# The rows of B and C of a selective scan: one tile and one load, or two

## The chip, the cores and the metric

The kernel runs on one core of a Trainium2 chip. The metric is the device time in microseconds (us). The engines are named as the profile names them: PE (matrix multiply), DVE (vector), ACT (scalar functions), POOL (GpSimd) and SP, whose queue issues most of the DMAs. Each engine works through its own queue in order, and waits on semaphores for what the other engines or DMAs have to deliver.

## The reference

Four layers run on 4 images of 64 x 64 tokens with 128 channels, all in 32-bit floats: a Mamba-like block with a selective scan in four directions (layer 0), self-attention over all tokens (layer 1), a convolution block (layer 2) and neighborhood attention with an MLP (layer 3). The change lies in the scan of layer 0:

```python
B, H, W, C = (4, 64, 64, 128)
DI, N, R, K = (256, 16, 8, 4)
xs = jnp.stack([x0, x1, x0[..., ::-1], x1[..., ::-1]], axis=1)      # four directions
x_dbl = jnp.einsum('bkdl,kcd->bkcl', xs, x_proj_w)
dts, Bs, Cs = jnp.split(x_dbl, [R, R + N], axis=2)
delta = jax.nn.softplus(jnp.einsum('bkrl,kdr->bkdl', dts, dt_w) + dt_b[None, :, :, None])
A = -jnp.exp(A_log).reshape(K, DI, N)
def step(h, t):
    x_t, d_t, B_t, C_t = t
    h = jnp.exp(d_t[..., None] * A) * h + (d_t * x_t)[..., None] * B_t[:, :, None, :]
    return (h, jnp.einsum('bkdn,bkn->bkd', h, C_t))
```

For each image and direction there are 256 channels x 16 states, each a linear recurrence over 4096 tokens. B scales what goes into the state, and C weighs the 16 states into the output.

## The kernel before, in words

The program is written for a framework that schedules it: it orders the instructions of every engine by priority and by a model of time, inserts the semaphores, and hands out tiles from pools. A tile name with bufs=4 has four buffers in turn; the instruction that writes the fifth tile waits for the last reader of the first.

**Inputs of the scan.** `scan_inputs` computes delta, du (delta times x, on POOL, L328) and the rows of B and C, and writes them to DRAM scratch: delta (L326), du (L332), and `D.bc` (L325), which holds for each of the 16 states n one row of B and one row of C of 512 tokens side by side (shape [16, 2, 512]).

**The scan.** `selective_scan` runs over an image. Its loops are, from outside in: the direction k (4, in the order 0, 1, 3, 2), the chunk of 512 tokens i (8), the half of the channels hf (2), the group of four states j (4), and pp (2). A tile has 128 partitions, 32 channels times 4 states. One pass of the innermost loop is a unit: 512 units in an image, 2048 in all. For each half, two dt tiles (delta) and two du tiles are loaded (L468, bufs=4), each copied to the four states. For each j, one bc tile is loaded (L476, bufs=4): B in its first 512 columns and C in its second, copied to the 32 channels. A unit is then:

- dB = du x B on POOL (L485), for two groups g of channels at once, into one of four buffers;
- for each g: dA = exp(delta A) on ACT into PSUM (L491, three buffers), and the recurrence on DVE (L493, tensor_tensor_scan), into dA or hc;
- the product with C: on DVE for each g (L498), or, in 5 of 16 units of the first image and in 7 of 16 of the others (`ON_POOL`), on POOL for both g at once (L506), put behind by two units (`BEHIND`, a list called `waiting`) so that POOL doesn't wait for the scan;
- the last column copied as the state for the next chunk, on ACT (L500, L502).

When both units of a j are made, PE sums over the states with a 128 x 32 matrix of ones (`pick`, L539) into py. At the first j of a half, py is begun with the skip term (L524, for which y_before is loaded from xc in two halves at L520) or with what earlier directions gave (L527 and L534, loads L526 and L530). At the last j ACT copies py to y_sum and stores it (L549 to L558).

**What runs beside it.** The scan of image b+1 has the highest priority. Beside it run the other layers of image b (`rest`: scan_output, layers 1 and 2, layer 3), and beside the first image's scan the inputs of the images to come. What is left of the last image runs when its scan is over. On each engine the instructions of both are in one queue.

Loads, of the scan and of the other layers, are issued by SP in one order. The load of a bc tile waits until its buffer's last reader, a product on DVE or POOL, is done; what stands behind it on SP waits too.

Of the kernel before, what the change touches and what calls it, by code (L numbers as in the profile page):

```python
# [28 lines left out]
F32 = mybir.dt.float32  # L29
# [13 lines left out]
LC = 512  # L43
# [20 lines left out]
def bc(ap, shape):  # L64
    return ap.to_broadcast(list(shape))


def mid(ap, n):

    return bc(ap.unsqueeze(1), [ap.shape[0], n, ap.shape[1]])  # L70


def span(c, n=LC):
    return slice(c * n, (c + 1) * n)
# [12 lines left out]
def after(tc, later, earlier, kind=mybir.DependencyClass.Sync):  # L87
    tc.add_manual_dep(
        later.ins, earlier.ins.name, mybir.DependencyInfo(kind, mybir.DependencyReason.DATA), reason="group"
    )  # L90
# [347 lines left out]
def selective_scan(tc, K, S, D, img):  # L438

    nc = tc.nc
    pool, psum = S.pool, S.psum
    waiting = []

    def settle(unit):
        while waiting and waiting[0][0] <= unit:
            waiting.pop(0)[1]()

    for k in ORDER:
        back = k >= 2
        order = slice(None, None, -1) if back else slice(None)
        last = 0 if back else LC - 1
        state = pool.tile([128, NJS, NPR, 2], F32, name="state")
        for i in range(NCH):  # L460
            c = NCH - 1 - i if back else i
            for hf in range(2):
                dts, dus = [], []
                for pp in range(2):
                    rows = span(2 * hf + pp, 32)
                    for name, src, out in (("dt", D.delta, dts), ("du", D.du, dus)):
                        t = pool.tile([128, 2, LC], F32, name=name, bufs=4)
                        nc.sync.dma_start(  # L468
                            t.rearrange("p g t -> p (g t)"),
                            src[img][k][c][rows].rearrange("d g t -> d (g t)").unsqueeze(1).to_broadcast([32, 4, 2 * LC]),  # L470
                        )
                        out.append(t)
                py = []
                for j in range(NJS):
                    bct = pool.tile([128, 2, LC], F32, name="bc", bufs=4)
                    nc.sync.dma_start(  # L476
                        bct.rearrange("p g t -> p (g t)"),
                        D.bc[img][k][c][4 * j : 4 * j + 4].rearrange("n w t -> n (w t)").unsqueeze(0)
                        .to_broadcast([32, 4, 2 * LC]),
                    )  # L480
                    hcs, made = [], []
                    for pp in range(2):
                        pr = 2 * hf + pp
                        dB = pool.tile([128, 2, LC], F32, name="dB", bufs=4)
                        nc.gpsimd.tensor_mul(dB, dus[pp], mid(bct[:, 0, :], 2))  # L485
                        on_pool = S.unit % 16 in ON_POOL[img > 0]
                        S.unit += 1
                        hc = pool.tile([128, 2, LC], F32, name="hc", bufs=6)
                        for g in range(2):
                            dA = psum.tile([128, LC], F32, name="dA", bufs=3)  # L490
                            nc.scalar.activation(dA, dts[pp][:, g, :], AF.Exp, scale=S.A[:, k, j, pr, g : g + 1])  # L491
                            hg = hc[:, g, :] if on_pool else dA
                            nc.vector.tensor_tensor_scan(  # L493
                                hg[:, order], dA[:, order], dB[:, g, order],
                                0.0 if i == 0 else state[:, j, pr, g : g + 1], ALU.mult, ALU.add,
                            )
                            if not on_pool:
                                mm = nc.vector.tensor_mul(hc[:, g, :], dA, bct[:, 1, :])  # L498
                                if i < NCH - 1:
                                    nc.scalar.copy(state[:, j, pr, g : g + 1], dA[:, last : last + 1])  # L500
                        if on_pool and i < NCH - 1:
                            nc.scalar.copy(state[:, j, pr, :], hc[:, :, last])  # L502
                        if on_pool:

                            def product(hc=hc, bct=bct, made=made):
                                made.append(nc.gpsimd.tensor_mul(hc, hc, mid(bct[:, 1, :], 2)))  # L506

                            waiting.append((S.unit + BEHIND, product))
                        else:
                            made.append(mm)  # L510
                        hcs.append(hc)
                        settle(S.unit)

                    def total(k=k, c=c, hf=hf, j=j, hcs=hcs, made=made, py=py):
                        if j == 0:
                            py.append(psum.tile([128, LC], F32, name="py"))
                            before = pool.tile([128, LC], F32, name="y_before", bufs=3)
                            if k == 0:
                                for pp in range(2):
                                    nc.sync.dma_start(  # L520
                                        before[span(pp, 64), :],
                                        D.xc[img][c][span(2 * hf + pp, 32)].rearrange("d g t -> g d t"),
                                    )
                                nc.tensor.matmul(py[0], S.skip[:, hf, :], before, start=True, stop=False)  # L524
                            elif k >= 2:
                                nc.sync.dma_start(before, D.y_first[img][k % 2][c][:, hf, :])  # L526
                                nc.tensor.matmul(py[0], K.ident, before, start=True, stop=False)  # L527
                            if k == 2:
                                cols = pool.tile([128, NCH, RC, RC], F32, name="y_before", bufs=3)
                                nc.sync.dma_start(  # L530
                                    cols.rearrange("p c a b -> p c (a b)"),
                                    D.y_cols[img][:, :, c, hf].rearrange("c p x -> p c x"),
                                )
                                nc.tensor.matmul(  # L534
                                    py[0].rearrange("p (a c b) -> p a c b", a=RC, b=RC), K.ident,
                                    cols.rearrange("p c a b -> p a c b"), start=False, stop=False,
                                )
                        for q in range(4):
                            mm = nc.tensor.matmul(  # L539
                                py[0][32 * q : 32 * q + 32, :], S.pick, hcs[q // 2][:, q % 2, :],  # L540
                                start=(k == 1 and j == 0), stop=(j == NJS - 1),
                            )
                            if q == 0:
                                for m in made:
                                    after(tc, mm, m)
                        if j == NJS - 1:
                            y = pool.tile([128, LC], F32, name="y_sum")
                            if k == 3:
                                nc.scalar.copy(  # L549
                                    y.rearrange("p (b a) -> p b a", b=H), py[0].rearrange("p (a b) -> p b a", b=H)  # L550
                                )
                                nc.scalar.dma_start(
                                    D.y_cols[img][c][:, :, hf, :], y.rearrange("p (r x) -> p r x", r=NCH)
                                )
                            else:
                                nc.scalar.copy(y, py[0])
                                to = D.y[img][c] if k == 2 else D.y_first[img][k % 2][c]
                                nc.scalar.dma_start(to[:, hf, :], y)  # L558

                    waiting.append((max([S.unit] + [w[0] for w in waiting]), total))  # L560
                    settle(S.unit)
    settle(S.unit + BEHIND)
# [1194 lines left out]
```

## Time and profile before

| | |
|---|---|
| device time, median of 3 runs | 8969.41 us (8967.38 to 8976.73) |
| the profiled execution | 8980.37 us |
| its span | 8978.6 us |
| busy PE / DVE / ACT / POOL | 7201.0 / 7114.0 / 5647.9 / 7046.0 us |
| mean rate of the DMAs | 176 GB/s |
| loads of bc (L476) | 1024 of 512 KB |
| loads of dt and of du (L468) | 512 of each, 512 KB |
| mean of a dB multiply (L485) and of a POOL product (L506) | 2363 ns each |
| mean of a DVE product (L498) | 677 ns |

The profile is of one execution. A row of a group has the line, the engine, the operation with its output and inputs, the count, the busy time in us with the mean in ns, and the idle time of the engine just before these instructions with what ended most of it. A row of waits has the waiting engine and line, what it waited for, the total in us, how often, and the longest. "SPq" is the issue of a DMA by SP's queue. A row of windows has the stretch in us, its length, the busy time of each engine with the instructions begun, the clock granted to PE, the share of time that the DMA engines were busy, and GB/s. A row of the timeline has the start and the duration in us, and in brackets the idle time of the engine before it and what ended it.

### The profile page before, as it was taken

The page shows a single profiled execution, that of the slowest core. Times are in us where ns is not written, and L with a number is a line of the kernel's source. Part 1 is how long each engine was busy: PE and PEld are TensorE (multiplying, and loading weights), DVE is VectorE, ACT ScalarE, POOL GpSimd, SP SyncE. Part 2 cuts the span into 40 slices and gives each one's busy share as a digit, 9 for nine tenths or more (in the row PEclk, how much of TensorE's full clock was granted, in tenths as well). Part 3 has the DMA queues.
Part 4 walks back from the last instruction along what each step waited for, and adds up shares of the span by engine and source line. Part 5 has one row for each costly group of instructions (what it writes and reads, how often), then busy time and mean ns, then how long its engine had stood idle before and what let it go on. Part 6 is the DMA issues. An engine that isn't in the chain of part 4 may idle for free. (4 is left out here: it accounts for less than half of the span.)

```text
span 8978.6 us, 99358 instructions
## 1 busy us (share of the span) xinstructions
PE 7201.0 (80%) x30116; PEld 2731.9 (30%) x30116; DVE 7114.0 (79%) x8483; ACT 5647.9 (63%) x11581; POOL 7046.0 (78%) x3064
## 2 busy tenths in 40 slices
PE   5835868686788997888788888777888988888987
PEld 2211213132422232334322233333222333343333
DVE  3888878787899989988899989888899889833433
ACT  5746767676666666657766666667666666564355
POOL 5988898999899979998799979988899889910000
PEclk8756878696889998888899988888899988899988
DMA  5777666777544446565444555565444455520020
GB/s 169 250 239 235 240 244 233 253 251 265 184 166 161 167 151 211 194 212 186 152 166 172 179 180 183 193 205 176 166 161 168 160 200 190 192 74 4 7 79 29
DMA packets 716655, 1581.74 MB, mean 176 GB/s; under 512 B 203317, under 2 KB 328396, under 8 KB 711757
## 3 DMA queue, kind: packets, MB, share of 16 engines
q1 hardware_dynamic: 585805, 1399.10, 45.7%
q10 hardware_dynamic: 130304, 176.19, 5.6%
q8 instruction: 241, 3.95, 0.2%
q14 instruction: 305, 2.50, 0.1%
HBM read 1280.47 MB, written 283.59 MB: 174 GB/s over the span
## 5 line engine op out<-in xcount | busy, mean ns | idle before, releaser
L485 POOL TENSOR_TENSOR dB<-du,bc 128x1024 f32<-128x1024 f32 x2048 | 4790.4, 2363 | 687.8 <-DMA bc<-bc_dram 238.9
L491 ACT ACTIVATE dA<-dt,w_A_log 128x512 f32<-128x512 f32 x4096 | 2783.0, 691 | 607.6 <-DVE hc L493 298.0
L493 DVE TENSOR_TENSOR_SCAN dA<-dA,state,dB 128x512 f32<-128x512 f32 x2128 | 2631.7, 1273 | 291.0 <-POOL dB L485 158.2
L493 DVE TENSOR_TENSOR_SCAN hc<-dA,state,dB 128x512 f32<-128x512 f32 x1456 | 1805.5, 1269 | 299.3 <-ACT dA L491 116.6
L506 POOL TENSOR_TENSOR hc<-hc,bc 128x1024 f32<-128x1024 f32 x832 | 1963.0, 2363 | 83.5 <-ACT state L502 59.2
L498 DVE TENSOR_TENSOR hc<-dA,bc 128x512 f32<-128x512 f32 x2432 | 1568.7, 677 | 127.5 <-PE py L539 111.8
L539 PE MATMUL py<-hc,pick 128*32 128x512 f32 x8192 | 1252.5, 690 | 385.6 <-POOL hc L506 279.7
L829 PE MATMUL pa<-e,l_v 128*128 128x512 f32 x2048 | 1080.8, 660 | 28.8 <-ACT e L785 28.6
L500 ACT COPY state<-dA 128x1 f32<-128x1 f32 x2128 | 329.0, 158 | 1219.0 <-DVE hc L498 1207.7
L781 PE MATMUL pair<-l_g,l_f 32*128 32x512 f32 x2048 | 540.5, 679 | 185.9 <-ACT e L785 133.0
L785 ACT ACTIVATE e<-pair 128x1024 f32<-128x1024 f32 (+1 forms) x448 | 508.3, 1135 | 228.6 <-PE pair L781 222.3
L829 PEld LDWEIGHTS pa<-e,l_v 128*128 128x128 f32 x2048 | 379.8, 202 | 694.7 <-issue 635.1
L539 PEld LDWEIGHTS py<-hc,pick 128*32 128x32 f32 x8192 | 212.6, 116 | 1146.2 <-issue 448.0
L1287 PE MATMUL pair<-table,ident 128*128 128x512 f32 x768 | 424.4, 680 | 114.3 <-ACT e L1297 93.9
L247 PE MATMUL ps<-band,w_conv_diag 128*128 128x504 f32 (+3 forms) x1152 | 500.0, 593 | 3.5 <-ACT delta L397 3.5
L493 DVE TENSOR_TENSOR_SCAN dA<-dA,dB 128x512 f32<-128x512 f32 x304 | 357.7, 1213 | 71.2 <-POOL dB L485 52.2
L328 POOL TENSOR_TENSOR du<-delta,xc 128x1024 f32<-128x1024 f32 x128 | 333.1, 2610 | 48.4 <-ACT delta L397 46.9
L201 PE MATMUL ps<-ident,ln_xn 128*128 128x128 f32 x512 | 135.5, 360 | 289.4 <-ACT ln_xn L198 213.3
L1297 ACT ACTIVATE e<-pair 128x1024 f32<-128x1024 f32 (+1 forms) x224 | 254.4, 1136 | 154.9 <-PE pair L1291 154.5
L219 PE MATMUL ps<-xnT,w_fc_w 128*128 128x512 f32 x512 | 276.2, 674 | 69.3 <-ACT mlp_h L226 24.4
L781 PEld LDWEIGHTS pair<-l_g,l_f 32*128 32x128 f32 x2048 | 141.7, 191 | 548.9 <-ACT e L785 272.3
L247 PEld LDWEIGHTS ps<-band,w_conv_diag 128*128 128x128 f32 x1152 | 221.5, 193 | 282.0 <-issue 262.6
(274 smaller groups left out, 8562.9 us busy)
## 6 DMA issues: line engine op xcount, KB each, us to landing
bc<-bc_dram SPq DMA_DIRECT2D x1024, 512.0 KB
dt<-delta_dram SPq DMA_DIRECT2D x512, 512.0 KB
du<-du_dram SPq DMA_DIRECT2D x512, 512.0 KB
delta_dram<-delta ACTq DMA_DIRECT2D x128, 512.0 KB
du_dram<-du SPq DMA_DIRECT2D x128, 512.0 KB
table<-biasT_dram SPq DMA_DIRECT2D x72, 512.0 KB
y_first_dram<-y_sum ACTq DMA_DIRECT2D x128, 256.0 KB
y_before<-y_first_dram SPq DMA_DIRECT2D x128, 256.0 KB
```

What stands on the lines that cost most here:

```text
L247: mm = nc.tensor.matmul(out[:, r0 - row0 : r1 - row0, c0:c1], lhsT((dy + 1) * 3 + dx + 1), src[:, r0 + dy : r1 + dy, c0 + dx : c1 + dx], s ...
L328: nc.gpsimd.tensor_mul(du.rearrange("p d (a b) -> p d a b", b=H), deltas[b].rearrange("p d (a b) -> p d a b", b=H), tk,)
L485: nc.gpsimd.tensor_mul(dB, dus[pp], mid(bct[:, 0, :], 2))
L491: nc.scalar.activation(dA, dts[pp][:, g, :], AF.Exp, scale=S.A[:, k, j, pr, g : g + 1])
L493: nc.vector.tensor_tensor_scan(hg[:, order], dA[:, order], dB[:, g, order], 0.0 if i == 0 else state[:, j, pr, g : g + 1], ALU.mult, ALU.add,)
L498: mm = nc.vector.tensor_mul(hc[:, g, :], dA, bct[:, 1, :])
L506: made.append(nc.gpsimd.tensor_mul(hc, hc, mid(bct[:, 1, :], 2)))
L539: mm = nc.tensor.matmul(py[0][32 * q : 32 * q + 32, :], S.pick, hcs[q // 2][:, q % 2, :], start=(k == 1 and j == 0), stop=(j == NJS - 1),)
L781: nc.tensor.matmul(ps[:, u, :], f[quad, t // 4, span(t % 4, 128)], g[quad, c, :], start=True, stop=True)
L785: made = nc.scalar.activation(e, ps, AF.Exp)
L829: nc.tensor.matmul(pa, v[:, 8 * q + t, :], es[q], start=(t == 0 and q == 0), stop=(t == 7 and q == 3),)
L1287: nc.tensor.matmul(ps[:, u, :], K.ident, t[:, u, :], start=True, stop=False)
```

## The change

B and C get a tile each, `b_rows` and `c_rows`, of 512 columns, with four buffers each, and a load each of 256 KB: B's first, then C's. The bytes in SBUF (four times 4 KB per partition) and the bytes moved stay as they were. dB reads b_rows; the products on DVE and POOL read c_rows. Both loads are on L478 of the changed kernel; the lines of dB, the scans and the products keep their numbers.

```diff
                 for j in range(NJS):
-                    bct = pool.tile([128, 2, LC], F32, name="bc", bufs=4)
-                    nc.sync.dma_start(
-                        bct.rearrange("p g t -> p (g t)"),
-                        D.bc[img][k][c][4 * j : 4 * j + 4].rearrange("n w t -> n (w t)").unsqueeze(0)
-                        .to_broadcast([32, 4, 2 * LC]),
-                    )
+
+                    bt, ct = (pool.tile([128, LC], F32, name=name, bufs=4) for name in ("b_rows", "c_rows"))
+                    for w, t in enumerate((bt, ct)):
+                        nc.sync.dma_start(
+                            t, D.bc[img][k][c][4 * j : 4 * j + 4, w, :].unsqueeze(0).to_broadcast([32, 4, LC])
+                        )
...
-                        nc.gpsimd.tensor_mul(dB, dus[pp], mid(bct[:, 0, :], 2))
+                        nc.gpsimd.tensor_mul(dB, dus[pp], mid(bt, 2))
...
-                                mm = nc.vector.tensor_mul(hc[:, g, :], dA, bct[:, 1, :])
+                                mm = nc.vector.tensor_mul(hc[:, g, :], dA, ct)
...
-                            def product(hc=hc, bct=bct, made=made):
-                                made.append(nc.gpsimd.tensor_mul(hc, hc, mid(bct[:, 1, :], 2)))
+                            def product(hc=hc, ct=ct, made=made):
+                                made.append(nc.gpsimd.tensor_mul(hc, hc, mid(ct, 2)))
```

## The prediction

> **What bounds the kernel now.** I read the windows by stage first, then the costliest groups, then the waits, then one stretch of the timeline. The chain that ended last is of little use here: it holds the tail after the scan (7888 to 8979 us, no POOL work), which the change does not touch.
>
> The windows give, after the seconds, the busy us of PE, weight load, DVE, ACT and POOL.
>
> ```profile
> 2250.00:3800.00 1550.00, 1309.61 (x5732) 483.53 (x5724) 1392.18 (x1624) 1006.71 (x2057) 1416.41 (x611) 0.89 0.51 175
> 3800.00:5400.00 1600.00, 1358.25 (x5674) 514.11 (x5672) 1410.76 (x1671) 1060.74 (x2172) 1425.41 (x615) 0.89 0.52 179
> 5400.00:7000.00 1600.00, 1316.68 (x5970) 487.30 (x5970) 1431.46 (x1671) 1053.31 (x2160) 1475.40 (x637) 0.88 0.53 179
> 7000.00:7888.00 888.00, 741.83 (x3556) 278.24 (x3552) 775.51 (x889) 543.89 (x1119) 789.37 (x341) 0.87 0.53 181
> 7888.00:8979.00 1091.00, 944.58 (x4376) 442.86 (x4372) 352.42 (x549) 558.10 (x841) 0.00 (x0) 0.92 0.12 38
> ```
>
> From 2250 to 7888 us POOL is busy 5106.6 of 5638 us (90.6%), DVE 5009.9 (88.9%), PE 4726.4 (83.8%). POOL is first, DVE close behind; DMA stands at half. POOL's work is two groups:
>
> ```profile
> L485 POOL TENSOR_TENSOR dB<-du,bc 128x1024 f32<-128x1024 f32 x2048 | 4790.4, 2363 | 687.8 <-DMA bc<-bc_dram 238.9
> L506 POOL TENSOR_TENSOR hc<-hc,bc 128x1024 f32<-128x1024 f32 x832 | 1963.0, 2363 | 83.5 <-ACT state L502 59.2
> ```
>
> Over the scan (88 to 7888 us) POOL is busy 7015 us and idle 785. In the waits the largest single cause is the bc load:
>
> ```profile
> POOL dB L485 <- DMA bc<-bc_dram: 238.9, 112, 9.3
> POOL dB L485 <- DVE hc L493: 196.6, 68, 24.7
> POOL dB L485 <- DVE dA L493: 95.9, 30, 21.0
> ...
> DVE dA L493 <- POOL dB L485: 210.5, 154, 9.1
> DVE hc L493 <- POOL dB L485: 84.6, 57, 6.1
> ```
>
> So POOL waits 292 us for DVE and DVE 295 us for POOL: they bind in turn. SP's own waits say why bc is late: its issue stands for the product that still reads the old tile.
>
> ```profile
> SPq L476 <- POOL hc L506: 1118.5, 348, 10.9
> SPq L476 <- DVE hc L498: 999.4, 310, 30.2
> ```
>
> One of the longer stalls, SP's rows and then POOL's, and a window inside it (last columns: DMA share and GB/s):
>
> ```profile
> 5983.46 2.73 SPq L520 DMA_DIRECT2D y_before<-xc_dram  x4
> 5986.29 1.22 SPq L476 DMA_DIRECT2D bc<-bc_dram  x1
> ...
> 6000.29 2.35 POOL L485 TENSOR_TENSOR dB<-du,bc 128x1024 f32<-128x1024 f32 x1 [7.66 <-DMA bc<-bc_dram]
> ```
>
> ```profile
> 5984.50:5988.00 3.50, 3.50 (x29) 3.07 (x28) 3.50 (x4) 2.04 (x4) 3.50 (x3) 0.92 0.10 40
> ```
>
> Four 128 KB loads move at 40 GB/s: 512 KB need 13 us, and the bc load behind them is awaited until 6000.29, 13 us after its issue ended. A load must be asked for early to be safe from this.
>
> **What the Trainium skill says.** "DMA: Bandwidth & Descriptors", under "Why a DMA increments its semaphore by 16 and not by 1": a DMA uses the largest number of engines, up to 16, that divides the slowest dimension of both sides. For the y_before load from xc that dimension is 2; the window's share of 0.10 of 16 engines agrees. The same page, "Queues, rings and completion order": each issuer owns one ring per engine, consumed in order. The 13 us above fit that. Its "Rules for kernel authors" advise few large transfers and call those under 64 KB mostly overhead; here 512 KB become twice 256 KB, above that mark. The trace's packet records give 159 ns for a 4096-byte packet and 84 ns for one of 2048 (medians), so halving costs little.
>
> **The change part by part.**
>
> *B's buffer comes free earlier.* Before, bc load number J may go when both dB multiplies (L485) and both products (L498, L506) of J-4 are done; after, B's load needs only the dB multiplies. From the order of the queues I counted, for every load, the dB multiplies that stand on POOL between the release (its own, or that of a dt, du or bc load ahead of it on SP) and the first use. Set beside the 112 stalls of the trace:
>
> ```
> dBs between   bc loads   stalled   us
> 0                32        12     17.9
> 1                97        47     76.0
> 2               234        35     91.9
> 3               317        16     50.5
> 4               244         2      2.5
> 5 or more       100         0      0
> ```
>
> One dB is 2.33 us from start to start, with a product between some of them. The program after has 6 for 920 of the 1024 B loads, 5 for 99, less for five. By the table the stalls fall to almost nothing: I leave 5 us, so **-234 us** of POOL idle.
>
> *C's load.* It goes out where bc's went, but is needed at the product. Counted in the same way to the first product (always on DVE), 47 loads have 2 or fewer dBs, 178 have 3, 515 have 4, 284 more. At the table's means (0.39, 0.16, 0.01 us) that is 18 + 28 + 8 = 54 us. DVE runs a dB and two scans (2.33 + 2.4 us) behind that count, which moves each load about one class down: some 5 to 10 us, plus loads caught behind y_before. Bounds 0 and 54, taken **+20**. Behind a product that waits on DVE stand the next scans, then ACT's state copies and exps, and PE's sums.
>
> *What takes over.* POOL can run only four dB tiles ahead of the scans. I followed each stall to the next wait: 61 of the 239 us are followed by POOL waiting for DVE before DVE ever waits for POOL (swallowed), 69 by DVE waiting for POOL (real), 108 by another bc stall (open). I call a third swallowed: **+80** of the 234; bounds 61 and 169.
>
> *More conditions.* 824 of the 832 products on POOL now wait for a DMA too, and dBs carry some 430 conditions more. A semaphore instruction on POOL has a median of 17 ns: 14 + 7 = 21 us at most, some behind the running multiply. Taken **+10**.
>
> *1024 more issues on SP* at 0.519 us (the bc issue's median) are 531 us of a queue that over the scan mostly waits. They delay the du, dt and y_before loads between them by 0.5 us each. du and dt are released 8 or 9 dBs ahead for nearly all, before and after, so that slack covers it; taken 0. Without it, 531 us would be the bound. *Packets:* 131,072 of 4096 bytes become twice as many of 2048: 9 ns more per pair, 1.18 ms over 16 engines, 74 us of share at 0.5 to 0.7. Covered by idle DMA; 0. Multiplies, scans and the tail keep shapes and counts: 0. The queues' order changes in small ways on every engine; POOL's other work stands at the same points of the scan as before. I give that nothing, and ±30 us.
>
> **Sum:** -234 + 20 + 80 + 10 = -124. The profiled execution took 8980.37 us (span 8978.6 and 1.8 around it), so 8856. The median of the runs, 8969.41, is 0.12% lower: 8856 x 0.9988 = **8845 us**, -1.4%.
>
> **The rivals.**
> *All of it, or more.* POOL is the only bound, and the time after a stall comes back too: -234 to 8735; with the DVE stalls that follow, 8700. For it: from 5400 to 7000 bc is 83.5 of POOL's 125 idle us. Against it: DVE at 88.9%.
> *Another engine takes it.* DVE and PE are the real bound: DVE waits 112 and 89 us for hc buffers that PE has not summed, and PE, busy 83.8%, reaches only 86.6% in the tail, where it runs the layers without the scan. If 85% is swallowed, -35: 8934. Against it: the 69 us that are certain.
> *The wait moves to C (slower).* SP serves in order, so C loads stand behind y_before and the added B loads, and each late one halts DVE's queue. If C waited as bc loads with 2 dBs did (0.39 us), 1024 loads cost 400; against 239 won that is +161, of which two thirds count: 9075. It decides from 0.23 us per load (239/1024). Against it: 799 of 1024 have 4 dBs or more.
> *The change does nothing.* If the order on SP put B's load always behind the C load four back, nothing would come sooner. Against it: B loads stand two or three tiles ahead of C's in 987 of 1024 cases.
>
> **How the numbers follow.** A measurement of this kernel tells about 0.2% (18 us) from no change. Likeliest, part regained (8800 to 8900): 0.50. Nearly all or more (below 8800): 0.22. Mostly swallowed, still visible (8900 to 8951): 0.13. Nothing visible: 0.06. Slower by C's waits: 0.09. Hence faster 0.85, same 0.06, slower 0.09. The range, 8740 to 8965, leaves out the full regain and the slower case, and takes in the +54 and the 169.
>
> **What would show it.** Right: the wait of POOL's dB for B falls below 20 us, POOL's waits for DVE rise from 292 towards 370, POOL's share from 2250 us to the scan's end rises from 90.6 to about 92%, and the scan ends near 7765. DVE's waits for c_rows stay under 54 us. Wrong: B's wait still above 60 us (early issue was not the cause); waits for C above 150 us; or B's wait gone with the time unchanged (DVE or PE bound).

## The result and the profile after

The changed kernel takes 8926.63 us (median of four runs, 8920.93 to 8938.2); the kernel before took 8973.07 us on the same chip. The ratio is 0.995, with a 95% interval of 0.9938 to 0.9961: 46 us are won, and the interval holds no value at or above 1. The forecast was 124 us. The profiled execution took 8928.4 us, 52 us less than the 8980.37 of before, with a span of 8926.7.

First the costliest groups of the page after (busy us, mean ns, idle us before, largest releaser), then POOL's waits (us, times, longest).

```profile
L485 POOL TENSOR_TENSOR dB<-du,b_rows 128x1024 f32<-128x1024 f32 x2048 | 4801.3, 2368 | 622.9 <-DVE hc L493 184.8
L506 POOL TENSOR_TENSOR hc<-hc,c_rows 128x1024 f32<-128x1024 f32 x832 | 1969.3, 2367 | 52.7 <-issue 23.9
L498 DVE TENSOR_TENSOR hc<-dA,c_rows 128x512 f32<-128x512 f32 x2432 | 1567.9, 676 | 115.0 <-PE py L539 97.5
```

```profile
POOL dB L485 <- DVE hc L493: 184.8, 64, 20.3
POOL dB L485 <- issue: 113.7, 44, 6.7
POOL dB L485 <- DVE dA L493: 76.8, 40, 6.7
POOL dB L485 <- PE py L539: 70.9, 14, 21.2
...
POOL dB L485 <- DMA b_rows<-bc_dram: 6.8, 3, 4.4
```

The wait for B has gone from 238.9 to 6.8 us. But the idle time ahead of dB has fallen only from 687.8 to 622.9. The labels "issue" and "PE py" hide where it went. A dB waits for a load, for POOL's own order, or for the scan that frees its dB tile; PE is none of these. POOL's row and then VectorE's rows of one such stall:

```profile
4145.31 4.68 POOL L485 TENSOR_TENSOR dB<-du,b_rows 128x1024 f32<-128x1024 f32 x2 [5.25 <-issue]
```

```profile
4138.25 0.67 DVE L630 TENSOR_TENSOR x<-x,pb 128x512 f32<-128x512 f32 x1
4139.02 1.13 DVE L632 SCALAR_TENSOR_TENSOR x<-pg,rstd,x 128x128 f32<-128x128 f32 x4
...
4142.72 2.45 DVE L493 TENSOR_TENSOR_SCAN hc<-dA,state,dB 128x512 f32<-128x512 f32 x2
```

VectorE works for another layer from 4138.25 on and starts the two scans at 4142.72; they end at 4145.17, and POOL's dB starts 0.14 us later. So its dB tile was freed by the scans, whatever the label says. I counted every stall of dB that ended within 0.2 us of the end of a scan: 148 stalls with 385 us before, 261 with 600 us after (by the labels, 292 and 262 us). All other stalls of dB fell from 301 to 22 us. So of 279 us that left one kind, 215 came back as the other. During those 600 us VectorE was running scans for 353, products for 42 and other layers for 86, and was idle for 119.

The windows after (busy us of PE, weight load, DVE, ACT, POOL, then clock, DMA share and GB/s):

```profile
2250.00:3800.00 1550.00, 1302.76 (x5822) 485.54 (x5822) 1416.52 (x1649) 1014.75 (x2072) 1431.75 (x618) 0.90 0.54 180
3800.00:5400.00 1600.00, 1365.52 (x5704) 505.18 (x5704) 1431.23 (x1690) 1071.95 (x2205) 1444.04 (x623) 0.89 0.54 181
5400.00:7000.00 1600.00, 1313.38 (x5984) 496.45 (x5980) 1427.12 (x1672) 1052.35 (x2162) 1481.62 (x639) 0.88 0.54 179
7000.00:7840.00 840.00, 707.92 (x3468) 268.89 (x3466) 722.40 (x834) 514.77 (x1056) 729.04 (x315) 0.89 0.54 179
7840.00:8927.00 1087.00, 936.79 (x4372) 441.03 (x4372) 353.78 (x553) 557.76 (x840) 0.00 (x0) 0.93 0.12 39
```

POOL is busy 5086.45 us from 2250 to the last row of the scan at 7804.4, or 91.6%. The scan thus ends 84 us earlier than before (the last y_sum copy, 7888.1 then), and its last dB starts 88 us earlier. This is in the summary of line L485, before and then after (ns min/median/max, first and last start in us):

```profile
L485 POOL TENSOR_TENSOR dB<-du,bc x2048: 2328/2359/2486, 119.4 to 7875.2; 128x1024 f32<-128x1024 f32 x187
```

```profile
L485 POOL TENSOR_TENSOR dB<-du,b_rows x2048: 2331/2362/2472, 111.4 to 7787.1; 128x1024 f32<-128x1024 f32 x187
```

The rest was lost after the scan. SP's rows at that point, before and then after: the last store of image 2's other layers (L1327), and the first load of the tail (L592), some 6.5 us behind it on the same queue.

```profile
7879.83 0.36 SPq L1327 DMA_DIRECT2D x_dram<-x  x1
...
7886.33 0.43 SPq L592 DMA_DIRECT2D y<-y_dram  x1
```

```profile
7838.57 0.38 SPq L1327 DMA_DIRECT2D x_dram<-x  x1
...
7845.06 0.43 SPq L592 DMA_DIRECT2D y<-y_dram  x1
```

The other layers ended only 41 us earlier. In each of the twelve kernels of this document that have layer 1 for every image, the tail's first load follows that store by 6.4 to 8.4 us, whether the scan ended before or after it: the end of the other layers decides when the tail starts. From the last dB to the tail's first load it was 11 us before and is 58 us after. From the last dB to the end of the span it was 1103.4 us and is 1139.6: 88 - 36 = 52.

One sentence of the description above is wrong: the scan has the lowest priority, not the highest. Its priority number (`SCAN_FIRST`, 10,000,000) is larger, and in this framework the smaller number goes first, so the other layers are placed first on every engine and the scan fills what they leave.

### The profile page after: what moved, and what is told of

Same layout as the page of the kernel before. It is cut to its first block, busy times and chain, and to the rows that moved or that the text cites. A ratio compares the mean times of both kernels' runs of the same rounds, so it can differ in the third digit from the quotient of the medians.

```text
span 8926.7 us, 101201 instructions
## 1 busy us (share of the span) xinstructions
PE 7138.8 (80%) x30116; PEld 2711.7 (30%) x30116; DVE 7119.8 (80%) x8483; ACT 5642.5 (63%) x11581; POOL 7048.6 (79%) x3064
## 2 busy tenths in 40 slices
DMA packets 864124, 1581.89 MB, mean 177 GB/s; under 512 B 219702, under 2 KB 344781, under 8 KB 859214
## 5 line engine op out<-in xcount | busy, mean ns | idle before, releaser
L485 POOL TENSOR_TENSOR dB<-du,b_rows 128x1024 f32<-128x1024 f32 x2048 | 4801.3, 2368 | 622.9 <-DVE hc L493 184.8
L493 DVE TENSOR_TENSOR_SCAN dA<-dA,state,dB 128x512 f32<-128x512 f32 x2128 | 2634.8, 1272 | 231.0 <-ACT dA L491 136.3
L493 DVE TENSOR_TENSOR_SCAN hc<-dA,state,dB 128x512 f32<-128x512 f32 x1456 | 1802.5, 1268 | 263.6 <-PE py L539 117.2
L506 POOL TENSOR_TENSOR hc<-hc,c_rows 128x1024 f32<-128x1024 f32 x832 | 1969.3, 2367 | 52.7 <-issue 23.9
L498 DVE TENSOR_TENSOR hc<-dA,c_rows 128x512 f32<-128x512 f32 x2432 | 1567.9, 676 | 115.0 <-PE py L539 97.5
L829 PE MATMUL pa<-e,l_v 128*128 128x512 f32 x2048 | 1062.0, 650 | 16.8 <-ACT e L785 16.2
L493 DVE TENSOR_TENSOR_SCAN dA<-dA,dB 128x512 f32<-128x512 f32 x304 | 356.2, 1213 | 76.2 <-POOL dB L485 57.4
L233 PE MATMUL ps<-mlp_h,w_fc_w 128*128 128x512 f32 x512 | 275.8, 683 | 42.6 <-ACT mlp_h L226 42.6
```

The source lines that it names most:

```text
L233: nc.tensor.matmul(po, P.w2[:, f, :], hT[:, f, :], start=(f == 0), stop=(x is None and f == NF - 1))
L485: nc.gpsimd.tensor_mul(dB, dus[pp], mid(bt, 2))
L493: nc.vector.tensor_tensor_scan(hg[:, order], dA[:, order], dB[:, g, order], 0.0 if i == 0 else state[:, j, pr, g : g + 1], ALU.mult, ALU.add,)
L498: mm = nc.vector.tensor_mul(hc[:, g, :], dA, ct)
L506: made.append(nc.gpsimd.tensor_mul(hc, hc, mid(ct, 2)))
L829: nc.tensor.matmul(pa, v[:, 8 * q + t, :], es[q], start=(t == 0 and q == 0), stop=(t == 7 and q == 3),)
```

## The experiments

Each pair below has one kernel built on the kernel before and one on the changed kernel, with the same edit. The two of a pair ran on the same chip, beside the same runs of the kernel before; only the two kernels with the faster y_before load ran on different chips. The ratios are against the kernel before on the same chip. The question at the start was what took almost two thirds of the removed wait (144 of 232 us at the last dB): VectorE's own load (theory A of the short scans) or something that its load does not touch (theory B there). The letters are each set's own. The edits are shown shortened.

**Is it the split, or the earlier release?** One bc tile as before, but filled by two loads of 256 KB.

```
-  nc.sync.dma_start(bct..., D.bc[..., 4*j:4*j+4] ... [32, 4, 2*LC])
+  for w in range(2):
+      nc.sync.dma_start(bct[:, w, :], D.bc[..., 4*j:4*j+4, w, :] ... [32, 4, LC])
```

> One part of the change alone: two loads of 256 KB, B first, but into the two halves of one bc tile, which comes free with the product as before. Theory A (what counts is the earlier release of B's buffer): POOL's wait for bc stays within 200 to 260 us, and the time is that of the kernel before or up to 0.3% longer for 1024 more issues; 8965 to 9000 us. Rival C (what counts is the smaller load of B that lands sooner): the wait falls below 120 us, and the time by 0.3 to 0.6%.

Measured: 8990.58 us, ratio 1.0015 (1.0006 to 1.0023). In POOL's waits of this kernel:

```profile
POOL dB L484 <- DMA bc<-bc_dram: 224.3, 93, 9.7
```

Theory A held, and rival C fell: the wait stays. The number and size of the loads do nothing good by themselves; the ratio is 0.15% above 1. That agrees with the Trainium skill, "DMA: Bandwidth & Descriptors", section "Rules for kernel authors", which advises few large transfers. What took the wait away is that B's tile has no product among its readers. SP's waits in the changed kernel say the same. The issue of the two loads now stands longest for dB, 1065 of these us ahead of B's load, where in the kernel before it stood 1118.5 us for POOL's product:

```profile
SPq L478 <- POOL dB L485: 1106.8, 604, 8.1
```

**Does VectorE take the rest?** The scans of units whose product is VectorE's own run on half their columns; the other columns of their result keep the decay factors. The products stay whole. The expectation under "Both relieved" says that they are cut too, which the edit does not do. A cut scan takes 741 ns on the mean in place of 1273.

```
+  cols = slice(None) if on_pool else slice(0, LC // 2)
-  scan(hg[:, order], dA[:, order], dB[:, g, order], ...)
+  scan(hg[:, cols][:, order], dA[:, cols][:, order], dB[:, g, cols][:, order], ...)
```

> The kernel before, with DVE relieved: in the units whose product is on DVE the recurrence (L493) runs over 256 of the 512 columns only, so the later columns keep the decay factors in place of states. 2432 scans lose some 0.6 us each, 1.46 ms of DVE time. It is the base for the changed kernel with the same cut. Theory A (the time that the early B gave was taken back by DVE, whose scans free the dB buffers): POOL's waits for DVE nearly vanish here, POOL's wait for bc stays at 200 us or more, and the time falls to about 8650 to 8800 us. Theory B (it was taken back by PE and by the order of the queues, not by DVE): the time falls little, since DVE was not what held POOL; above 8850 us.

> The changed kernel with the same cut of the recurrence (256 of 512 columns in the units whose product is on DVE). Theory A: with DVE relieved the early B is worth what it saves POOL, so this kernel is faster than the kernel before with the same cut by at least 150 us (1.7%), three times the 46 us of the full kernels. Theory B: the difference stays near 46 us (0.5%).

Measured: 8778.67 us and 8698.43 us, ratios 0.9785 (0.9764 to 0.9806) and 0.969 (0.9671 to 0.971). The pair differs by 80 us. The last dB starts at 7661.0 and 7641.1, only 20 us apart, though 179 us of waits for bc (185.0 to 5.8) are gone. The profiled executions are 67 us apart, and the other 47 come after the last dB: the tail's first load goes out 34 us behind it in one and 57 us ahead of it in the other. The 80 us lie between the marks of both theories, and POOL's stalls behind scans did not vanish (255 us in the kernel before with this cut, 471 in the changed one). VectorE's load alone did not swallow the gain: with VectorE relieved the scan gained even less.

**Do the other layers take it?** Layer 1 is left out for the three images that run beside the scan.

```
-  layer1(tc, K, A, D, img, xT, wide)
+  if wide:
+      layer1(tc, K, A, D, img, xT, wide)
```

> Leaves layer 1 out for the three images that run beside the scan (the last image keeps it), so that PE, ACT and the other layers have much less to do there; one tile for B and C as before. It is one half of a pair with the kernel of the next run; what counts is the difference. The time itself should fall to about 8700 to 8900, since POOL still sets the scan's pace in this kernel (its wait for bc stays at 200 us or more). The other layers should end well over 100 us ahead of the scan.

> The same without layer 1 beside the scan, with B and C in tiles of their own. Theory A (the other layers take the gain back: they keep PE, ACT and VectorE from the scan, and in the end finish after it): the pair differs by 100 us or more, since the other layers now end first and the scans come less late; POOL's waits for scans stay well under the 600 us of the changed kernel. Theory B (VectorE's own load takes the gain, whatever runs beside): the pair differs by 30 to 60 us as the full kernels do (46). In between, near 84 us: only the finish behind the scan's was lost to the other layers, the scan's own gain was not.

Measured: 8951.18 us, ratio 0.9972 (0.9961 to 0.9982), and 8853.79 us, ratio 0.9859 (0.9839 to 0.9878). The pair differs by 97 us. The summaries of L485 in the two:

```profile
L485 POOL TENSOR_TENSOR dB<-du,bc x2048: 2327/2355/2417, 116.6 to 7873.7; 128x1024 f32<-128x1024 f32 x187
```

```profile
L485 POOL TENSOR_TENSOR dB<-du,b_rows x2048: 2329/2362/2464, 113.3 to 7777.1; 128x1024 f32<-128x1024 f32 x187
```

Taking layer 1 away moves the last dB by 1.5 us in the kernel before and by 10 us in the changed one. But the clock granted to PE changes too: from 3800 to 5400 us it is 0.77 in the kernel before without layer 1 (the row below), where it was 0.89 with it. The sums over the states take longer, first with layer 1 and then without:

```profile
3800.00:5400.00 1600.00, 1056.76 (x4804) 396.45 (x4802) 1380.25 (x1631) 960.86 (x2069) 1404.76 (x607) 0.77 0.52 177
```

```profile
L539 PE MATMUL py<-hc,pick 128*32 128x512 f32 x8192 | 1252.5, 690 | 385.6 <-POOL hc L506 279.7
```

```profile
L539 PE MATMUL py<-hc,pick 128*32 128x512 f32 x8192 | 1480.5, 817 | 1594.6 <-POOL hc L506 1452.6
```

So it is not shown that layer 1 costs the scan nothing; the scan has less beside it, but slower sums. Within the pair the clocks are alike (0.77 and 0.76), and the difference of 97 us can be read. At the end the other layers are now far ahead: the tail's first three loads go out long before the last dB (the first by 362 and 354 us), the fourth 20 and 16 us after it, and the whole gain of the scan (97 us) shows in the time. This settles one half: **the scan gained some 90 us in the full kernel too, and 36 of them were lost because other layers ended last.** It is the middle case of the expectation (near 84 us). Two marks missed: the kernel before was to take 8700 to 8900 us, and the changed kernel's stalls behind scans, at 594 us, are not well under 600.

**Both relieved.** Layer 1 left out, and the short scans (both edits above).

> One half of a pair: one tile for B and C; layer 1 left out beside the scan, and VectorE's scans and products cut to half their columns where the product is VectorE's own. So both VectorE and PE have time to spare in the scan, and only POOL is loaded as before. POOL's wait for bc should stay at 180 us or more and set the pace; the difference to the next kernel is what counts.

> The same with B and C in tiles of their own. Theory C (what took 180 of the removed 279 us is VectorE's and PE's load together: with one of them relieved the other holds the scan): with both relieved the last dB starts 150 us or more earlier than in the pair's other half, and POOL's stalls behind scans fall below 350 us. Theory D (the loop itself does it: four dB tiles, six hc tiles and products put behind, whatever the load): the last dB again starts only 20 to 100 us earlier, as in the three pairs so far (88, 96 and 20).

Measured: 8727.69 and 8648.25 us, ratios 0.9728 (0.9714 to 0.9741) and 0.9636 (0.9623 to 0.9649); last dB at 7652.2 and 7562.7. The gain at the last dB is 90 us again (79 in the medians), of 155 us of waits removed. Theory C fell: it asked for 150 us, and for stalls behind scans below 350 us, which are 438. PE's sums are slow here too (820 ns), but PE mostly stands for POOL's product, as the row of the changed kernel of this pair says:

```profile
L540 PE MATMUL py<-hc,pick 128*32 128x512 f32 x8192 | 1485.4, 820 | 1525.8 <-POOL hc L507 1494.5
```

So the loads of VectorE and PE are not the answer, as far as these cuts relieve them.

**More dB tiles.** Five dB tiles, paid for once by a b_rows and a y_before tile, and once by a dt tile.

```
-  dB = pool.tile([128, 2, LC], F32, name="dB", bufs=4)
+  dB = pool.tile([128, 2, LC], F32, name="dB", bufs=5)      # after_dB5: b_rows 3, y_before 2
                                                            # after_dt3_dB5: dt 3
```

> The changed kernel with five dB buffers in place of four; the room comes from b_rows (three buffers) and y_before (two). Theory A1 (POOL's waits for the scans come from uneven work on DVE that four dB tiles can't bridge): the waits of dB for scans fall from about 600 to 450 us, and the time by some 40 to 80 us against the changed kernel, to about 8860. Theory A2 (DVE is at its limit on average, with what it waits for from ACT and PE): one more buffer only fills once; 8910 to 8940 us. B's three buffers leave four multiplies of lead, which should still hide the load.

> The changed kernel with five dB tiles in place of four and three dt tiles in place of four, for the memory. Theory of the short ring (POOL can only stand four units ahead of VectorE, so each late scan stops it): POOL's waits for scans fall from about 600 us to under 450, the scan's last dB starts 60 us or more earlier than 7787, and the time falls by 20 us or more if the other layers do not then hold it. Theory of the other layers: the time stays within 20 us of 8927 whatever POOL gains, since the store that ends image 2's other layers (7839) does not come earlier. Against both: with three dt tiles ACT may wait for dt, which would show as waits of ACT for dt loads of over 50 us.

Measured: 9221.94 us, ratio 1.0277 (1.0259 to 1.0295), and 9230.59 us, ratio 1.0279 (1.0262 to 1.0295). Both cost some 300 us against the changed kernel, whatever paid for the tile: the opposite of what I expected. POOL's stalls behind scans rose from 600 us to 695 and 792 in place of falling. In VectorE's waits of the second kernel:

```profile
DVE hc L498 <- PE py L539: 309.4, 133, 8.5
```

That was 97.5 us with four tiles. VectorE has no hc tile to write into, since PE has not yet summed the old ones.

**The ring without layer 1.** Three and five dB tiles, in pairs.

> One half of a pair: the kernel before without layer 1 beside the scan, five dB tiles for four and three dt tiles for four. Theory of the ring: POOL's waits for scans fall, its waits for bc stay at 200 us or more or rise, and the difference to the next kernel is above the 97 us of the pair with four: 120 us or more. Cause that the ring does not touch: it stays between 80 and 115 us.

> The other half, B and C in tiles of their own, five dB tiles. Theory of the ring: the last dB starts 25 us or more ahead of the 7777 us with four tiles, and the waits for scans are lower. Cause that the ring does not touch: within 20 us of 7777. The 300 us that five dB tiles cost the changed kernel with layer 1 should not come back here if they came from the order in which the other layers were placed.

> The kernel before without layer 1 beside the scan, with three dB tiles for four. Theory of the ring: POOL waits more for scans than for bc, and the difference to the next kernel is under 70 us. Cause that the ring does not touch: 80 to 115 us as with four.

> The other half, B and C in tiles of their own, three dB tiles. Theory of the ring: later than with four by 60 us or more, and closer to its partner (under 70 us) than with four (97 us). Cause that the ring does not touch: 80 to 115 us ahead of its partner.

Measured, in that order: 9007.58, 9022.42, 8864.54 and 8815.71 us, with ratios of 1.0037 (1.0025 to 1.0048), 1.0048 (1.0031 to 1.0065), 0.9879 (0.986 to 0.9897) and 0.9818 (0.9802 to 0.9834). The theory of the ring fell as I had put it: fewer tiles are faster, and with five the change wins nothing. Of its marks for the pair with three only two came true, that POOL waits more for scans than for bc and that the pair differs by less than 70 us (49). What goes with it is visible in POOL's timeline. A stretch of the kernel before, and one of the changed kernel:

```profile
4010.80 7.01 POOL L485 TENSOR_TENSOR dB<-du,bc 128x1024 f32<-128x1024 f32 x3
4018.12 2.44 POOL L485 TENSOR_TENSOR dB<-du,bc 128x1024 f32<-128x1024 f32 x1 [0.31 <-DVE hc L493]
4020.52 2.35 POOL L506 TENSOR_TENSOR hc<-hc,bc 128x1024 f32<-128x1024 f32 x1
4024.57 2.35 POOL L506 TENSOR_TENSOR hc<-hc,bc 128x1024 f32<-128x1024 f32 x1 [1.70 <-ACT state L502]
4032.04 2.35 POOL L506 TENSOR_TENSOR hc<-hc,bc 128x1024 f32<-128x1024 f32 x1 [5.12 <-ACT state L502]
4035.99 13.93 POOL L485 TENSOR_TENSOR dB<-du,bc 128x1024 f32<-128x1024 f32 x6 [1.60 <-DMA bc<-bc_dram]
```

```profile
3978.43 2.37 POOL L506 TENSOR_TENSOR hc<-hc,c_rows 128x1024 f32<-128x1024 f32 x1
3980.75 4.68 POOL L485 TENSOR_TENSOR dB<-du,b_rows 128x1024 f32<-128x1024 f32 x2
3985.36 2.38 POOL L506 TENSOR_TENSOR hc<-hc,c_rows 128x1024 f32<-128x1024 f32 x1
3987.68 4.69 POOL L485 TENSOR_TENSOR dB<-du,b_rows 128x1024 f32<-128x1024 f32 x2
```

Here the kernel before lets three products of POOL catch up ahead of a dB that waits for its bc. In the stretch of the changed kernel no dB waits, and dB and product alternate at a fixed distance. Which instruction stands behind which on POOL is the scheduler's choice, made before the run. I counted, along the whole timeline of POOL in images 1 to 3, how many later units' dB run before a unit's product (the **lead**): 3.46 on the mean before, 3.89 after. For all pairs, the lead, the wait for bc or b_rows and the start of the last dB. "Won" is how much earlier the last dB starts, "removed" is what left POOL's wait for B:

```
pair                      wait for B, us    lead            last dB, us          won   of removed
full                      238.9 ->   6.8    3.46 -> 3.89    7875.2 -> 7787.1      88      232
short scans               185.0 ->   5.8    3.45 -> 3.92    7661.0 -> 7641.1      20      179
no layer 1                219.0 ->   9.6    3.44 -> 3.90    7873.7 -> 7777.1      97      209
no layer 1, short scans   175.0 ->  20.5    3.43 -> 3.92    7652.2 -> 7562.7      90      155
no layer 1, 3 dB           54.3 ->   1.0    2.89 -> 2.90    7781.0 -> 7737.0      44       53
no layer 1, 5 dB          368.1 ->  14.2    3.76 -> 4.89    7918.6 -> 7942.8     -24      354
y_before in 32 rows       171.4 ->  10.5    3.46 -> 3.89    7841.0 -> 7756.9      84      161
```

Where the lead stays (three tiles), 44 of 53 us arrive. Where it grows by 0.4 to 0.5, 65 to 159 us are lost. Where it grows by 1.1, all 354 are. Within the five pairs in the middle the loss does not follow the lead (0.43 goes with 144 and with 77 us, 0.49 with 65). In the changed kernels the lead is 0.1 below the number of dB tiles (2.90, 3.89, 4.89): the dBs stand as far ahead as the tiles let them. A product that stands later holds its hc tile and its c_rows tile longer. With five tiles that shows directly: VectorE's waits for py in its scans and products (L493 and L498) rise from 190 us to 461 within the pair, against 78 to 73 with three.

**The same cure in the full changed kernel.** Three dB tiles, and then a seventh hc tile in the memory of the fourth dB.

```
-  dB ... bufs=4        hc ... bufs=6
+  dB ... bufs=3        hc ... bufs=6      # after_dB3
+  dB ... bufs=3        hc ... bufs=7      # after_dB3_hc7
```

> The changed kernel, all layers, with three dB tiles for four; POOL's products stand 2.90 dB behind in place of 3.89. Theory of the late product: VectorE's waits for PE's py (216 us in the two groups) fall to under 100 us, the last dB starts 30 us or more before 7787, and the time falls by 30 us or more. Theory of the other layers alone: POOL gets a shorter ring and nothing else changes for the better; the last dB is not earlier, and the time is at 8927 or above.

> The same with seven hc tiles for six, in the memory of the fourth dB. Theory of the late product: the same wait for PE to free hc falls further, below 50 us, and the time is at or below that of the run before. If hc's ring had not been what the late product cost, this run equals the one before within 10 us, apart from what the other layers' placing moves (up to 50 us in the runs so far, seen in the wait between the last dB and the tail).

Measured: **8857.8 us**, ratio 0.9868 (0.9851 to 0.9884), and 8862.04 us, ratio 0.9869 (0.9852 to 0.9886). Both beat the two kernels; they are the fastest whole kernels here. VectorE's waits for py fall as the theory says, from 216 us to 83 and 14; the rows of L498 in the two:

```profile
DVE hc L498 <- PE py L539: 47.7, 22, 7.9
```

```profile
DVE hc L498 <- PE py L539: 10.9, 7, 6.6
```

The last dB was a miss and a hit: 7779.8, only 7 us earlier, with six hc tiles, and 7722.4, 65 us earlier, with seven. So in the full kernel the shorter lead alone did not bring the scan's loss back. The seventh hc tile, at the same lead (2.90), moved the last dB by 57 us; with three dB tiles, then, hc tiles did hold the scan, as the waits for py (83 to 14 us) also say. No run has seven hc tiles and four dB tiles. The first kernel won its time at the end: the tail's first load goes out 138 us ahead of the last dB, and the span ends 1075.7 us after that dB, as in the pair without layer 1 (1085.0 and 1080.3). In the second they ended last again (the tail's first load comes 56 us after the last dB), and the 1146.4 us after it ate what the scan had won. That is why the two times are within 10 us of each other, which by itself is what the expectation gave for the case that hc's ring does not matter.

**A faster load of y_before.** The first direction's load from xc, cut so that its slowest dimension is 32 and not 2.

```
-  nc.sync.dma_start(before[span(pp, 64), :], D.xc[img][c][span(2*hf+pp, 32)].rearrange("d g t -> g d t"))
+  for g in range(2):
+      nc.sync.dma_start(before[span(2*pp+g, 32), :], D.xc[img][c][span(2*hf+pp, 32), g, :])
```

> The changed kernel with the first direction's load into y_before cut so that its outer row count is 32 and not 2, same bytes. In the trace of the changed kernel this load keeps two DMA engines for some 13 us, and the loads for B and C behind it on the queue wait. If that delay is what makes VectorE wait for PE's py (216 us in two groups), the time falls by 20 us or more; if PE is late because of the other layers ahead of it on its queue, the time stays within 10 us of 8927.

> The kernel before with the first direction's y_before load cut so that its outer row count is 32 and not 2. If the 47 us that this cut gave the changed kernel come from the loads for B and C getting through sooner on the queue, the same cut gives the kernel before 40 us or more, since there POOL waits 239 us for that data. If they come from elsewhere in the changed kernel (PE's py, the other layers ending sooner by another order), it gives 0 to 20 us here.

Measured: on the changed kernel 8879.76 us, ratio 0.989 (0.9873 to 0.9907); on the kernel before 9028.65 us, ratio 1.0058 (1.0045 to 1.0072). The same edit wins 47 us on one and loses 51 on the other. Yet the last dB comes 30 and 34 us earlier. The difference lies in the other layers: the tail's first load comes 34 us after the last dB in one and 94 us in the other. Neither expectation had this. The 47 us pass the mark of 20, but not for its reason: VectorE's waits for py stay at 207 us (216 without the cut). It is a second case in which a time can't be read without asking which of the two chains ended last.

**Six products in 16 on POOL in place of seven, images 1 to 3.**

```
-  ON_POOL = ((1, 4, 7, 10, 13), (0, 2, 4, 6, 9, 11, 13))
+  ON_POOL = ((1, 4, 7, 10, 13), (0, 3, 6, 8, 11, 14))
```

> The changed kernel with six in place of seven of every 16 products on POOL for the images after the first: 96 products of 2.37 us, 227 us, leave POOL, and 192 half products of 0.68 us, 130 us, come to VectorE. If VectorE is by now as much the limit as POOL (theory A of the first runs), the time goes up by 50 us or more and POOL's waits for scans rise by 250 us or more; if POOL is still the limit, it falls by 50 us or more.

Measured: 9280.24 us, ratio 1.0337 (1.0323 to 1.0351). The 227 us taken from POOL win nothing: the last dB starts 144 us later, at 7931.3, and the tail's first load only 275 us after that. POOL's stalls behind scans rise from 600 to 911 us. Both marks of theory A came true, which fits VectorE as a limit beside POOL in the changed kernel; but the other layers ended later by 361 us too, so their new order may have its part in it.

## Why the prediction was wrong in its size

The direction was right and the time lies in the range, but the gain of the profiled execution is 52 us and not 124. It lies where the prediction saw "mostly swallowed, still visible" (0.13), not where it put its 0.50. Of the 72 us that are missing, 34 were lost in the scan, in the term "what takes over", and 36 in the tail, which the sum put at nothing. That the range still held the result is in part luck: no term of it stood for the tail. Step by step:

- **B's buffer comes free earlier (-234): right.** 232 us of the wait are gone, and the one-tile kernel shows that the early release did it.
- **C's load (+20): too large.** By the labels VectorE's products have no wait for c_rows, and POOL's have 2.6 us. The mark "under 54 us" held, and the slower rival with it fell. No run separates the 10 us for more conditions.
- **"What takes over" (+80): the first step that failed, by its size.** With the C term and the conditions I had +110 against the -234 in the scan; at the last dB it is +144 (232 - 88). The mechanism, POOL waiting for the scan that frees a dB tile, is there, and with little left for C the term itself is some 130 to 144, inside its bounds of 61 and 169. I had followed each old stall to the next wait of the old trace. That can't show what a new order brings. The 292 us that POOL was said to wait for DVE were read from the labels, which miss a part. So the mark "from 292 towards 370" can't be read from them either (they fell to 262); by the ends of the scans the waits rose from 385 to 600.
- **The order of the queues, given nothing and ±30: wrong.** On POOL the dBs are placed earlier against the products: the lead grew by 0.43 of a dB. In the pairs the loss is small where the lead stays and takes all where it grows most. What part of the 144 us it makes here is not shown.
- **The tail, 0: the second step that failed, by 36 us.** Its instructions did keep their shapes and counts, but the sum took for granted that its start follows the scan. In the kernel before the other layers ended 9 us ahead of the scan, which the prediction does not weigh. In the changed kernel they ended 34 us after it.

The account of the 52 us is then -232 in POOL's wait for B, +144 before the last dB and +36 after it. The mark "the scan ends near 7765" missed by 39 us (7804.4); POOL's share came out at 91.6% against 92.

The rival "Another engine takes it" came nearest in size (8934), but not for the reason it gave. With layer 1 gone and the scans short the scan still gained only 90 us, and PE stood for POOL's product.

What is shown: the early release, the loss at the end, and that over the pairs no growth of the lead, a middle one and a large one go with a small, a middle and a large loss. What is not shown: that the lead makes the loss. No run changed the order and nothing else, and the number of dB tiles changes the ring as well. The direct sign, VectorE's waits for py, falls by 5 us with three tiles and rises in the other six pairs, but not in step with the loss: by 271 us with five tiles, by 146 and 98 with the short scans, and by only 16 in the full pair, which lost 144. So the cause of the scan's loss stays open in part. Why five tiles cost as much as 300 us with layer 1 also stays open.

## What to carry to other kernels

Ahead of a forecast, look at what ends last now and by how much: two chains of work that end 9 us apart will not both move when one is made faster. When a wait is taken from one instruction of an engine, ask where a scheduler will now place that instruction, and what other work on the same engine falls behind it and may hold its buffers longer. More buffers in a ring aren't always better: here one dB tile less (8857.8 us) beat one tile more (9230.59 us, with a dt tile less), though most of what the first won over four tiles came at the tail.

## What I had not expected of the hardware

- Cutting a load in two costs little here. The loads' packets rose from 716,655 to 864,124 in all, and the share of the DMA engines on SP's queue from 45.7% to 47.0%. The two loads alone cost 0.15% of the whole kernel.
- POOL's multiplies are 5 ns longer on the mean in the changed kernel (2363 to 2368 ns for dB, 2363 to 2367 for products), 17 us over the 2880 of them. No run tells why.
